# Pre-LN attention and mixture of experts on one core: late small clears, more places for w1, results in larger pieces, and another start of the first sequence

## The chip, the cores and the metric

One Trainium2 chip, of which the kernel uses one core. The metric is the device time of one execution in microseconds; a comparison takes the median of several runs. Five engines work side by side, each through its own instructions in order: PE (matmul), DVE (vector), ACT (scalar), POOL (GpSimd) and SP, which here only issues DMAs. A DMA is issued by SP, ACT or POOL and lands later; whoever needs its data waits for its semaphore.

## The reference

Eight sequences of 512 tokens of width 128 go through one attention layer and one mixture of experts, both with a layernorm ahead and a residual behind.

```python
x = x + attn(layernorm(x), Wq, Wk, Wv, Wo, bo)   # 16 heads of 8, causal softmax
x = x + ffn(layernorm(x), gate_w, w1, b1, w2, b2)
# ffn: probs = softmax(x @ gate_w.T); the best 2 of 8 experts for each token
#      hidden = relu(x @ w1[e] + b1[e])   (128 -> 512)
#      out_e  = hidden @ w2[e] + b2[e]    (512 -> 128)
#      y = sum over the two experts of prob * out_e
```

All arrays are float32.

## The kernel before

**Order of the work.** Seven generators (`setup`, `project`, `shifts`, `attend`, `route`, `experts`, `sums`) each yield the time at which their next step is due, in units of one sequence; a loop at the end always runs the generator that is due first. The order so written is kept on PE, ACT, DVE and SP (`ORDERED`); POOL's order is left to the scheduler. An engine that waits holds up everything written behind it. On SP, ACT and PE nothing overtakes.

**Attention.** For sequence b, `project` (yield b - 1.7 on) does the layernorm, q and k, and splits both into three bf16 parts (`part`). The parts go to DRAM (`to_dram`, L378) and come back arranged by head (`pack`, L390) into `q2_buf[b % 2]` and `k2_buf[b % 2]` (trace names q and k), 24 rows a part, so that a bf16 matmul over 72 rows gives scores of float32 quality. For b = 0 this is done in four groups of four heads. For each group SP issues two q writes and three q packs, ACT one k write, POOL three k packs; on SP the order is write q, pack q, group after group. For later sequences it is one group, all on SP.

`shifts` takes, for each group g of four heads, the scores (L479, with the mask added at L489) in six units of one or two PSUM tiles, DVE takes the maximum of each tile's rows (L502), and the negated maximum, as two bf16 parts, is transposed (L446), copied (L450) and put by a DMA into two more rows of q2 (L456), for b = 0 on ACT's queue, later on SP's. `attend` then computes the scores again with keys as rows (L635; now with the shift in them), exponentials on ACT (L641), the causal zeroes by POOL's affine select (L647), and the products with v (L565).

**Dummy matmuls.** `keep_warm(k)` issues matmuls of 128x256 on a zero tile whose result nobody reads: 40 while the first input is loaded, and 75 (L129) behind the first sequence's v.

**Routing.** `route` chooses the experts of a sequence and gives each token and choice a slot in `xs[k]`, a DRAM array with room for each of the eight experts; `scatter` (L900) writes the normalised rows there with eight indirect DMAs of POOL. Sequences 0 to 6 are group k = 0, sequence 7 is group 1. `dispatch` is called after sequences 1, 3, 5, 6 and 7 and gives out the tiles of 128 slots that are certain to be full (steps 0 to 2) or all that remain (steps 3 and 4). A row that was never written must look empty: the whole of `xs[1]` and the spare part of `xs[0]` are cleared in `setup`; in `xs[0]` the 640 rows (`NEW`) behind each expert's fill are cleared after sequence 5 (L880 to L891), eight DMAs of SP. The scatters that come after wait for them.

**Experts.** The five steps have 8, 16, 16, 23 and 15 tiles; "tile 3.5" is tile 5 of step 3. For each four tiles SP gathers the rows (`gather`, L1050), and for each tile it fetches the expert's w1, b1 and b2 as one row of 644 words a partition (`fetch_to`, L973, 322 KB). PE transposes (L1081), multiplies by w1 (ph, L1120), ACT and DVE add b1 and take relu (L1127, L1129), PE multiplies by w2 (py, L984), DVE adds b2 (yo, L988), and POOL stores each row to `ys[k]` at its token's place (L1019). Tiles whose four are due before 8 have w1 in five buffers (`wt`), the 42 later ones in six places in the q of even sequences, with four fetched ahead.

**Sums.** When all stores of a group have landed, `sums` loads two rows of results for each token (L1173, 256 KB a DMA, into the q of odd sequences), adds them, weighted, to x (L1199) and stores x (L1155). For group 0 the first three sequences are loaded at once, that is six DMAs; the next ones follow the sums.

Of the kernel before, what the change touches and what calls it, by code (L numbers as in the profile page):

```python
# [9 lines left out]
F32 = mybir.dt.float32  # L10
# [8 lines left out]
P = 128  # L19
# [5 lines left out]
def preln_attn_moe(ctx: ExitStack, tc: tile.TileContext, x, wq, wk, wv, wo, bo,  # L25
# [35 lines left out]
    nc = tc.nc  # L61
# [10 lines left out]
    LEAD = 0.55  # L72
    WARM = (40, 75)
    XB = 3
# [33 lines left out]

    NEW = 2 * P if len(GROUPS[0]) == 1 else T + P
    ROOM = (len(GROUPS[0]) * T + P, T)  # L110
# [10 lines left out]


    idle_bf = const.tile([P, 2 * P], BF16, tag="idlebf", name="idle_bf")
    V.memset(idle_bf, 0.0)

    def keep_warm(k):
        idle = ps_mm.tile([P, T], F32, tag="mm", name=f"idle_{k}")
        for _ in range(WARM[k]):
            nc.tensor.matmul(  # L129
                idle[:, : 2 * P], lhsT=idle_bf[:, :P], rhs=idle_bf, start=True, stop=True  # L130
            )
# [87 lines left out]
    def setup():  # L219
# [13 lines left out]
        for k in range(2):  # L233
# [3 lines left out]
            )  # L237
        for t in (place_no, token):
            nc.gpsimd.iota(
                t, pattern=[[P, t.shape[1]]], base=0, channel_multiplier=1,  # L240
                allow_small_or_imprecise_dtypes=True,
            )
# [76 lines left out]
    def project():  # L319
# [13 lines left out]
        arrange(0, G)  # L333
        keep_warm(0)
        for b in range(B):
# [47 lines left out]
            def pack(s, g):  # L383

                src = (q_parts, k_parts)[s]
                heads = H // src.shape[0]
                for r in range(3):
                    o = r if s == 0 else 0
                    place = (q2_buf, k2_buf)[s][b % 2][24 * r : 24 * r + 24, ts(g, heads)]
                    (nc.gpsimd if b == 0 and s == 1 else nc.sync).dma_start(  # L390
                        out=place,
                        in_=src[g, o : o + 3].rearrange("c d h t -> (c d) h t"),
                    )
# [10 lines left out]
            if b > 0:  # L404
                to_dram(0, 0)
                yield b - 1.18
                to_dram(1, 0)
            else:

                for g in range(G):  # L410
                    for s in range(2):
                        to_dram(s, g)
                        pack(s, g)
                yield b - 1.18
# [22 lines left out]
            if b == 0:  # L437
                keep_warm(1)


    def shifts():
# [20 lines left out]
        for b in range(B):  # L462
            for g in range(G):
# [6 lines left out]
                for pr in range(2):  # L470
                    n = 2 * g + pr
                    for i, unit in enumerate(S_UNITS):
                        yield t0 + (3 * pr + i) / 24
                        for v, bank in enumerate(unit):
# [23 lines left out]
                            else:  # L498
                                top, src = pm[:, :, pr, 8], ps.rearrange(
                                    "p (u k) -> p u k", u=2  # L500
                                )
                            nc.vector.tensor_reduce(top, src, AX.X, ALU.max)  # L502
                        if late:
                            late.pop(0)()
# [295 lines left out]
    def dispatch(s, soon):  # L800
# [66 lines left out]
        if not last:  # L867
# [6 lines left out]
            else:  # L874
                given[k] = const.tile([P, E], F32, tag=f"given{k}", name=f"given_{k}")
                V.tensor_copy(given[k], taken)
        if len(GROUPS[k]) > 1 and b == GROUPS[k][-2]:

            fill = small.tile([1, E], I32, tag="fill", name=f"fill_{s}", bufs=1)
            V.tensor_tensor(fill, pc[0:1, :E], room[k][0:1, :E], ALU.add)  # L880
            yield soon(3)
            found = [
                nc.values_load(
                    fill[0:1, e : e + 1], engines=[mybir.EngineType.SP],
                    min_val=e * ROOM[k], max_val=(e + 1) * ROOM[k] - NEW,
                    skip_runtime_bounds_check_because="an expert has room for all tokens",
                )
                for e in range(E)
            ]
            for e in range(E):  # L890
                nc.sync.dma_start(  # L891
                    out=xs[k][bass.ds(found[e], NEW)].rearrange("(p a) d -> p a d", p=P),
                    in_=empty.unsqueeze(1).to_broadcast([P, NEW // P, XROW]),
                )

    def scatter(k, b, t):
        sent = []
        for i in range(NT):
            for j in range(2):
                ins = nc.gpsimd.indirect_dma_start(  # L900
                    out=xs[k],
                    out_offset=bass.IndirectOffsetOnAxis(
                        ap=slot[b][:, j * NT + i : j * NT + i + 1], axis=0
                    ),
                    in_=xn2[b][:, i, :], in_offset=None,
                )
                in_order(ins)
                for other in sent + [a for o in GROUPS[k] if o < b for a in scatters[o]]:
                    tc.declare_no_dep(
                        ins.ins, other, reason="every token and choice has its own slot"  # L910
                    )
                for other in gathers[k]:
                    tc.declare_no_dep(
                        ins.ins, other, reason="no slot of a tile given out is written"
                    )
                sent.append(ins.ins)
                if (i, j) != (NT - 1, 1):
                    t += 0.045 if b == B - 1 else 0.055
                    yield t
        scatters[b] = sent  # L920

# [7 lines left out]
    def experts():  # L929
        tiles = [(s, i) for s, step in enumerate(STEPS) for i in range(step[2])]  # L930
        wt, yo, at, xg, to, expert = {}, {}, {}, {}, {}, {}

        spare_q = q2_buf[0].rearrange("p h t -> p (h t)").bitcast(F32)
        spare_k = k2_buf[0].rearrange("p h t -> p (h t)").bitcast(F32)
        WTS, XGS = H * T // 2 // WROW, H * T // 2 // (4 * XROW)
        fetched = [0, 0, 0]
# [6 lines left out]
        def after(s, i):  # L943
            return when(s, quad(s, i)[0]) >= B

        def ahead(s, i):
            return WTS - 2 if after(s, i) else 3

# [3 lines left out]
        def fetch_to(n):  # L952
            while fetched[0] < min(n, len(tiles)):
# [11 lines left out]
                if after(s, i):  # L965
                    wt[s, i] = spare_q[:, ts(fetched[1] % WTS, WROW)]
                    fetched[1] += 1
                else:
                    wt[s, i] = work.tile(
                        [P, WROW], F32, tag="wt", name=f"wt_{s}_{i}", bufs=5  # L970
                    )
# [63 lines left out]
        def gather(s, i):  # L1035
# [13 lines left out]
            for j in range(m):  # L1049
                ins = nc.sync.dma_start(  # L1050
                    out=t[:, j, :], in_=xs[k][bass.ds(found[j], P)]
                )
                assert all(o in scatters for o in GROUPS[k] if o <= b)
                for o in GROUPS[k]:
# [34 lines left out]
        def loads():  # L1089
            t = 0  # L1090
            for s, i in quads:
                t = max(t, when(s, i + 1) - (0.22 if after(s, i) else 0.28))
                yield t
                while s not in row_no or STEPS[s][1] not in scatters:
                    t += 0.01
                    yield t
                gather(s, i)
# [51 lines left out]
    def sums():  # L1149
# [10 lines left out]
        for k, group in enumerate(GROUPS):  # L1160
# [5 lines left out]
            def load(n):  # L1166
# [5 lines left out]
                for j in range(2):  # L1172
                    ins = (nc.scalar if last and j else nc.sync).dma_start(  # L1173
                        out=y[:, j],
                        in_=ys[k][j * NTOK + n * T : j * NTOK + (n + 1) * T].rearrange(
                            "(c p) d -> p c d", p=P
                        ),
# [9 lines left out]

            yield t
            for n in range(min(3, len(group))):
                load(n)  # L1190
            if not last:
                t += 0.05
            for n, b in enumerate(group):
                y = ys_sb[n]
                for c in range(NT):
                    t += 0.05 if last else 0.013
                    yield t
                    for j in range(2):
# [3 lines left out]
                        )  # L1202
                    store(0)
                    if c == 0 and n > 0 and n + 2 < len(group):
                        load(n + 2)
# [52 lines left out]
```

## Time and profile before

| | us |
|---|---|
| median of 14 runs | 646.41 |
| lowest and highest | 644.95, 650.56 |
| profiled execution | 645.77 |
| its span | 644.0 |
| PE, DVE busy in the span | 565.6, 435.3 |
| ACT, POOL busy in the span | 305.4, 291.2 |
| mean granted PE clock | 0.927 |

A timeline line gives start, duration, engine, source line, operation, output and input tile, and how many; in brackets stands the idle time of the engine before it and what ended it. SPq and ACTq are the issues of DMAs. PEclk is the clock granted to PE, as a share of full speed. In a table of windows each engine has its busy time and the number of its instructions.

### The profile page before, as it was taken

Reading aid. Unit: us, or ns where it says so; the run is one execution under the profiler, and the core shown is the slowest. Engines: PE = TensorE matmul, PEld = TensorE weight load, DVE = VectorE, ACT = ScalarE, POOL = GpSimd, SP = SyncE. Lnnn points to the kernel's source line nnn. Section 1 sums busy time; section 2 is a strip of 40 time slices with the busy share of each in tenths; the row PEclk is TensorE's granted clock in tenths of the full one; section 3 lists DMA queues with packets and bytes.
Section 4 is the critical chain, followed back from the end, with each engine's and each line's share of the span. In section 5 each row is a group of like instructions: output and inputs, shape, how many; then the busy total and the mean of one; then the engine's idle time right before and its main releaser. Section 6 shows DMA issues by size and latency. Waiting matters only on the chain. (4 is left out here: it accounts for less than half of the span.)

```text
span 644.0 us, 13373 instructions
## 1 busy us (share of the span) xinstructions
PE 565.6 (88%) x4312; PEld 365.7 (57%) x4312; DVE 435.3 (68%) x1410; ACT 305.4 (47%) x679; POOL 291.2 (45%) x480
## 2 busy tenths in 40 slices
PE   8788999999899998989899998998388989999680
PEld 6434445435445454655556664665246779999670
DVE  4476577897798978788798866897165245433484
ACT  3135366556465565545545654554145433544230
POOL 3523242445456334645654465352435643764241
PEclk9779599999899999999999998999679998999796
DMA  2546337537825704722552374229522563887893
GB/s 73 177 129 140 64 116 149 165 116 168 180 86 124 185 26 110 180 64 79 135 130 66 119 170 128 68 68 149 114 75 81 156 204 94 254 232 241 248 306 95
DMA packets 77096, 87.95 MB, mean 137 GB/s; under 512 B 10796, under 2 KB 62164, under 8 KB 76020
## 3 DMA queue, kind: packets, MB, share of 16 engines
q1 hardware_dynamic: 70676, 75.85, 46.5%
q0 software_dynamic: 5120, 10.56, 5.2%
q8 instruction: 35, 0.57, 0.4%
q10 hardware_dynamic: 1232, 0.69, 0.4%
q14 instruction: 33, 0.27, 0.1%
HBM read 61.14 MB, written 28.22 MB: 139 GB/s over the span
## 5 line engine op out<-in xcount | busy, mean ns | idle before, releaser
L502 DVE TENSOR_REDUCE pm<-s 128x1 f32<-128x512 f32 (+2 forms) x320 | 206.9, 682 | 65.1 <-PE s L489 64.5
L641 ACT ACTIVATE pt<-st 128x512 f32<-128x512 f32 x320 | 178.1, 599 | 114.9 <-PE st L635 99.7
L647 POOL TENSOR_SCALAR_AFFINE_SELECT pt<-pt 128x256 f32<-128x256 f32 x256 | 101.6, 410 | 197.1 <-ACT pt L641 190.9
L479 PE MATMUL s<-k,q 72*128 72x512 bf16 (+3 forms) x512 | 119.9, 314 | 9.9 <-ACT pt L641 4.5
L565 PE MATMUL po<-pt,va 128*9 128x512 f32 (+3 forms) x1024 | 109.2, 454 | 7.5 <-POOL pt L647 7.4
L635 PE MATMUL st<-q,k 74*128 74x384 bf16 (+3 forms) x512 | 110.4, 313 | 5.1 <-DVE pm L502 2.8
L1019 POOL DMA_INDIRECT ys<-yo,to x78 | 75.5, 968 | 69.8 <-DVE x L1199 23.0
L984 PE MATMUL py<-w_sb,hT 128*128 x624 | 86.6, 285 | 0.4 <-ACT hT L1127 0.4
L479 PEld LDWEIGHTS <-q 72*128 72x128 bf16 x512 | 47.8, 101 | 68.8 <-issue 53.5
L489 PE MATMUL s<-mask_bf,ident_bf 128*128 128x256 bf16 (+1 forms) x320 | 84.0, 262 | 0.0
L984 PEld LDWEIGHTS py<-w_sb,hT 128*128 128x128 f32 x624 | 79.4, 200 | 4.1 <-issue 2.3
L900 POOL DMA_INDIRECT xs<-xn_f,slot x64 | 62.5, 977 | 27.2 <-issue 13.2
L635 PEld LDWEIGHTS <-k 74*128 74x128 bf16 x512 | 46.9, 102 | 28.7 <-issue 15.1
L565 PEld LDWEIGHTS po<-pt,va 128*9 128x9 f32 x1024 | 24.1, 90 | 65.7 <-issue 30.9
L1127 ACT ACTIVATE hT<-ph,q 128x128 f32<-128x128 f32 x126 | 37.1, 365 | 49.3 <-PE ph L1120 41.9
L1120 PE MATMUL ph<-xgT,q 128*128 128x128 f32 x336 | 47.0, 286 | 11.5 <-DMA q<-wrows 11.1
L1120 PE MATMUL ph<-xgT,wt 128*128 128x128 f32 x288 | 41.7, 290 | 12.2 <-DMA wt<-wrows 12.2
L1120 PEld LDWEIGHTS ph<-xgT,q 128*128 128x128 f32 x336 | 42.4, 199 | 13.9 <-DMA q<-wrows 8.9
L1120 PEld LDWEIGHTS ph<-xgT,wt 128*128 128x128 f32 x288 | 36.5, 199 | 17.0 <-DMA wt<-wrows 12.8
L1129 DVE TENSOR_SCALAR hT<-ph,q 128x128 f32<-128x128 f32 x42 | 14.7, 350 | 42.5 <-ACT hT L1127 41.4
L489 PEld LDWEIGHTS <-ident_bf 128*128 128x128 bf16 x320 | 32.4, 101 | 3.9 <-issue 2.1
L1129 DVE TENSOR_SCALAR hT<-ph,wt 128x128 f32<-128x128 f32 x72 | 20.2, 342 | 19.8 <-PE ph L1120 19.8
(155 smaller groups left out, 604.0 us busy)
## 6 DMA issues: line engine op xcount, KB each, us to landing
q<-wrows SPq DMA_DIRECT2D x42, 322.0 KB
wt<-wrows SPq DMA_DIRECT2D x36, 322.0 KB
q<-qparts SPq DMA_DIRECT2D x21, 384.0 KB
k<-kparts SPq DMA_DIRECT2D x21, 384.0 KB
q<-ys SPq DMA_DIRECT2D x15, 256.0 KB
k<-xs SPq DMA_DIRECT2D x42, 65.0 KB
qparts<-part SPq DMA_DIRECT2D x7, 384.0 KB
kparts<-part SPq DMA_DIRECT2D x7, 384.0 KB
```

Source lines behind the costliest of these rows:

```text
L479: nc.tensor.matmul(ps[:, at : at + (t + 1) * P], lhsT=q2[:KS, 2 * n + u, ts(t, P)], rhs=k2[:KS, 2 * n + u, : (t + 1) * P], start=(at == 0) ...
L489: nc.tensor.matmul(dst, lhsT=ident_bf, rhs=mask_bf if i > 0 else mask_bf[:, 0, :], start=False, stop=True, skip_group_check=True,)
L502: nc.vector.tensor_reduce(top, src, AX.X, ALU.max)
L565: nc.tensor.matmul(po[32 * h : 32 * h + VC, j * P :], lhsT=va[:, j, HG * g + h, :], rhs=at_cols(pts[pr], unit, u, at, W), start=(first and ...
L635: nc.tensor.matmul(ps[:, at : at + T - j * P], lhsT=k2[: KS + 2, 2 * n + u, ts(j, P)], rhs=q2[: KS + 2, 2 * n + u, j * P :], start=(at == ...
L641: nc.scalar.activation(pt[:, v, :], ps, AF.Exp, scale=SCALE)
L647: selects[0] = nc.gpsimd.affine_select(out=d, in_=d, pattern=[[0, 2], [1, P]], compare_op=ALU.is_ge, fill=0.0, base=0, channel_multiplier=-1,)
L900: ins = nc.gpsimd.indirect_dma_start(out=xs[k], out_offset=bass.IndirectOffsetOnAxis(ap=slot[b][:, j * NT + i : j * NT + i + 1], axis=0), ...
L984: nc.tensor.matmul(py, lhsT=hT[:, c, :], rhs=w2_sb[:, bass.ds(at[s, i] + c * E * D, D)], start=(c == 0), stop=(c == FC - 1),)
L1019: ins = nc.gpsimd.indirect_dma_start(out=ys[k], out_offset=bass.IndirectOffsetOnAxis(ap=to[s, first][:, i - first : i - first + 1], axis=0 ...
L1120: nc.tensor.matmul(ph[:, ts(c, P)], lhsT=wt[s, i][:, ts(c, P)], rhs=turned[s, first][:, ts(i - first, P)], start=True, stop=True,)
L1127: nc.scalar.activation(hT[:, c, :], ph[:, ts(c, P)], AF.Relu, bias=bias)
```

## The change

It has five parts.

1. **Clears.** The clears of 640 rows for each expert after sequence 5 are gone. After sequence 6, the last of group 0, 128 rows behind each expert's fill are cleared. They are declared free of any order against the scatters of group 0, in both directions. On SP they stand between the w1 fetches of tiles 2.4 and 2.5.
2. **Places for w1.** The 42 late tiles have twelve places: six as before and six in the k of odd sequences. Up to nine are fetched ahead, a count that grows from four by one with each tile.
3. **Results.** A token's row in `ys` is now 4p + c for token c * 128 + p, so that a load reads 2048 bytes in one piece for each partition, where it read four of 512. `token` is made to match.
4. **Sums.** Two sequences are loaded first, in two steps of their own, and the others two ahead of the sums; for group 0 one store is held back. On SP the first result load now stands behind the w1 fetch of tile 4.10; before, it stood behind that of tile 4.5.
5. **The first sequence.** All its packs are issued by SP, in the order: the q writes of groups 0 and 1, packs of q and k of group 0, the q write of group 2, packs of group 1, and so on; ACT issues the k writes as before. After each unit of `shifts` that is due before time 0 four dummy matmuls follow: eleven units, 44 matmuls.

POOL's order, which the scheduler makes, differs in few places: four scatters of sequence 5 stand among the selects that they stood behind, and the rstd of sequences 2 and 6 comes behind two selects, or one, that it came ahead of.

```diff
-    NEW = 2 * P if len(GROUPS[0]) == 1 else T + P
...
-        for t in (place_no, token):
+        for t, by_tile, by_row in ((place_no, P, 1), (token, 1, NT)):
             nc.gpsimd.iota(
-                t, pattern=[[P, t.shape[1]]], base=0, channel_multiplier=1,
+                t, pattern=[[by_tile, t.shape[1]]], base=0, channel_multiplier=by_row,
...
-                    (nc.gpsimd if b == 0 and s == 1 else nc.sync).dma_start(
+                    nc.sync.dma_start(
...
                 for g in range(G):
+                    to_dram(1, g)
+                to_dram(0, 0)
+                for g in range(G):
+                    if g + 1 < G:
+                        to_dram(0, g + 1)
                     for s in range(2):
-                        to_dram(s, g)
                         pack(s, g)
...
+                        if t0 + (3 * pr + i) / 24 < 0:
+                            keep_warm(WARM[2], f"{g}_{pr}_{i}")
...
-        if len(GROUPS[k]) > 1 and b == GROUPS[k][-2]:
+        if k == 0 and last:
...
-            yield soon(3)
+            yield soon()
...
             for e in range(E):
-                nc.sync.dma_start(
-                    out=xs[k][bass.ds(found[e], NEW)].rearrange("(p a) d -> p a d", p=P),
-                    in_=empty.unsqueeze(1).to_broadcast([P, NEW // P, XROW]),
-                )
+                ins = nc.sync.dma_start(out=xs[k][bass.ds(found[e], P)], in_=empty)
+                for other in [a for o in GROUPS[k] for a in scatters.get(o, ())]:
+                    tc.declare_no_dep(
+                        ins.ins, other, reason="these slots are no token's"
+                    )
+                cleared.append(ins.ins)
...
-        WTS, XGS = H * T // 2 // WROW, H * T // 2 // (4 * XROW)
+        HALF, XGS = H * T // 2 // WROW, H * T // 2 // (4 * XROW)
+        WTS = 2 * HALF
...
-            return WTS - 2 if after(s, i) else 3
+            if not after(s, i):
+                return 3
+
+            late = [a for a in tiles if after(*a)].index((s, i))
+            return min(WTS - 3, WTS // 2 - 2 + late)
...
-                            "(c p) d -> p c d", p=P
+                            "(p c) d -> p c d", p=P
...
-            yield t
-            for n in range(min(3, len(group))):
+            for n in range(min(2, len(group))):
+                yield t
                 load(n)
-            if not last:
-                t += 0.05
+                t += 0.0 if last else 0.03
...
-                    store(0)
-                    if c == 0 and n > 0 and n + 2 < len(group):
+                    store(0 if last else 1)
+                    if c == 1 and n + 2 < len(group):
```

## The prediction

> **What bounds the kernel now.** I read the page's slices first, then busy time by windows of 4 us, then the timeline, SP's queue alone, at each place where PE is idle, and last the order of instructions of both kernels engine by engine.
>
> The slices (16.1 us each; rows PE, PEclk, DMA):
>
> ```profile
> PE   8788999999899998989899998998388989999680
> ...
> PEclk9779599999899999999999998999679998999796
> DMA  2546337537825704722552374229522563887893
> ```
>
> From 90 to 445 us PE is busy nine tenths at full clock, and no part of the change works there. Three places stand out: the start (PEclk 7, 7, 9, 5), slice 29 (PE 3, DMA 9) and the end.
>
> Slice 29, in the timeline:
>
> ```profile
> 435.08 10.90 SPq L891 DMA_DIRECT2D xs<-empty  x8
> ...
> 446.10 3.24 SPq L456 DMA_DIRECT2D q<-nmT  x2
> ...
> 449.60 1.91 SPq L973 DMA_DIRECT2D wt<-wrows  x3
> ...
> 457.66 2.07 PE L1120 MATMUL ph<-xgT,wt 128*128 128x128 f32 x8 [9.14 <-DMA wt<-wrows]
> ...
> 457.89 0.97 POOL L900 DMA_INDIRECT xs<-xn_f,slot  x1 [11.51 <-DMA q<-nmT]
> ...
> 464.41 0.87 PE L565 MATMUL po<-pt,va 128*9 128x256 f32 x4 [2.97 <-POOL pt L647]
> ```
>
> Eight clears hold SP for 10.9 us. The shift rows behind them (their nmT is done at 432.61) go out at 446.10, the w1 behind those at 449.60, and PE waits 9.14 us for it. POOL's scatters of sequence 5 wait for the clears to land, until 457.89; selects queue behind the scatters, and PE waits for one again (2.97 us).
>
> The end:
>
> ```profile
> 595.10 4.39 SPq L1173 DMA_DIRECT2D q<-ys  x6
> ...
> 599.75 1.10 SPq L973 DMA_DIRECT2D q<-wrows  x2
> ...
> 604.41 2.08 PE L1120 MATMUL ph<-xgT,q 128*128 128x128 f32 x8 [6.10 <-DMA q<-wrows]
> ```
>
> SP stands before the first result load until the last store of group 0 has landed, issues six loads, and only then tile 5's w1. PE is idle from 598.31 to 604.41 and runs at half clock to 608.
>
> The start:
>
> ```profile
> 11.75 8.35 PE L129 MATMUL idle<-idle_bf 128*128 128x256 bf16 x75
> ...
> 17.73 6.22 POOL L390 DMA_DIRECT2D k<-kparts  x12
> ...
> 22.67 0.38 PE L479 MATMUL s<-k,q 72*128 72x512 bf16 x1 [2.56 <-DMA k<-kparts]
> ```
>
> The dummies end at 20.10, the first scores wait for k until 22.67. The granted clock then is a half in three stretches: 24.3 to 34.5, 41.4 to 48.2 and 61.8 to 78.9.
>
> **The start, -5.5 us.** The order of SP becomes: q writes of groups 0 and 1, q and k packs of group 0, q write of group 2, and so on: 12 packs more on SP, 12 fewer on POOL. SP's q write goes out at 12.92, the first q pack at 14.73, the third ends at 17.35 (rows as now). Three k packs at 0.39 us each (a group of three takes 1.12 to 1.18) end by 18.7; the q write of 17.62 was landed by 20.72, 2.3 us after its end, so k lands near 20.9 and the first scores come 1.7 us earlier. Later groups: 24 packs and 4 writes at 0.4 us are 11 us more, to about 30; scores of group 1 need theirs at 31. Hence the packs are covered; behind them on SP stand x2 and the small loads (now 32.57), which come earlier too.
>
> Dummies: 11 units (t0 below 0: six of group 0, five of group 1) get 4 matmuls, 44 x 0.111 us (75 took 8.35) = 4.9 us of PE. They lie in DVE's shadow: 10 maxima of 0.606 us are 6.06 us a group (the row at 35.65), PE's own score work 3.2 us at full clock (twice 22.67 to 24.3) plus 2.7 us of dummies 5.9. Each dummy tile takes a ps_mm buffer, so it waits for ACT or DVE to have read the tile three before; by the order these readers are done, and I take 0 (at most 1 us each for the three that wait on ACT).
>
> Followed through at full clock: DVE runs unbroken from first scores to xn of sequence 1 (5.3 us as now), scores and q projections, which at half clock took 28.5 to 36 us, are no longer PE's limit, and nh of group 0 ends near 31.0 instead of 34.05. nmT's row DMA, now at 36.57, is then at 33.6: -3.0. From 41.4 to 47.6 PE is busy without a break at half clock; at full clock that is 3.1 us shorter, of which I take 2.5, since DVE is busy 3.48 us of 40 to 44. Sum -5.5, bounds 0 and -9. The third half-clock stretch I leave as it is: its cause (PE 70% busy in 58.4 to 61.8, 1.0 us of it idle behind a maximum) is not touched, though the order now puts two selects ahead of the rstd that blocked POOL until 61.59.
>
> The fall at 24.3 came after a stretch of 3.4 us in which PE was 48% busy with no pause over 1.8 us, the one at 61.8 with no pause over 1.0 us. The Trainium skill (TensorE: Matmul & The Clock Gate, Part 1) has the clock fall only after an idle window of about 3.4 us; by that the dummies would fill pauses that cost nothing. The rows speak against it, and it is a rival below.
>
> **The large clears go, -14.7 us.** From 448.3 to 468.66 PE executes what is 5 us of work at full clock (busy time times PEclk: 1.2, 1.2 and 2.1 us in the windows from 456, 460 and 464, and 0.5). Without the clears: the shift rows go at 432.7, w1 at 434, so ph runs at 448.4 and not 457.66; the scatters, which the order now puts between the selects before, are done by 450, so the select behind 464.41 runs near 450.9 and po near 451.4 (-13.0); what follows to 468.66 ran at half clock (3.4 us, -1.7). What is late next is the gate chain at 472 (PE 1.84 of 4 us), which moves along. Bounds: 9.1, the plain stall, and 16.
>
> **The small clears come, +2.5 us.** Eight of 128 rows, behind the w1 of tile 2.4 (third step, tile 4). In today's times: DVE's fill after rowno, 495.1; the eight register loads took from 432.25 to 435.08, 2.8 us; the issues as xs gathers of the same size (1.89 us for four) 3.8 us: to 501.6. Behind them wait w1 of 2.5 (now 491.0), landing near 504.4, against ph at 503.06: 1.4 us; then the gather, which now waits for the clears to land (503.8), then w1 of 2.6, landing near 508.6 against 506.35 plus 1.4: 2.3 us in all. POOL, whose scatters do not wait for these, goes on. Bounds 0 (PE idles 1.7 us between 508 and 520 anyway) and +6.
>
> A price by rows supports this: 5120 packets of 520 bytes become 1024. The Trainium skill (DMA: Bandwidth & Descriptors, Bandwidth) has a 64 KB transfer at 0.95 us, which for eight would be an estimate of 7.6 us of transfer; the sum would be 3 us worse. No row has this clear alone.
>
> **Twelve places for w1, -1.5 us.** PE idles 2.7 us from 540 to 596 (sum over the windows), mostly for w1. Up to nine ahead instead of four removes most: -1.5, bounds 0 and -3. The second six places lie in k of odd sequences, free after sequence 7's last st at 513.80; the first write there is behind the row at 524.65, so it waits for nothing.
>
> **The end, -7.0 us.** By the new order the first result load stands behind the w1 of tile 4.10, not 4.5. That place is free when tile 3.21 is done (591), before the stores land (594.98). So PE goes on at 598.3. Next late is DVE: from relu of tile 4.5 to that of 4.14 its queue has 42 sums, 9 relus, 9 yo and 10 small ones; by starts in the rows at 611 to 616 a pair of sums takes 0.65, a relu 0.26, a yo 0.20, a small one 0.19: 13.7+2.3+1.8+1.9 = 19.7 us, against PE's 9 x 1.79 + 0.9 = 17.0. From 599.0 that gives 618.7 for the relu now at 627.12: -8.4. The loads must keep up: 8.9 MB moved in 595 to 628, less five w1 (1.6 MB) now fetched earlier, is 7.3 MB in 23 us, 317 GB/s, where the best windows show 333 to 341. So I take -6 (bounds -2 and -8.4). The last ys load, 634.30 to 638.5, has 128 rows a load instead of 512: -1.0, bounds 0 and -2 (half its 4.2 us pass before data flows fast). The out stores of sequences 5 and 6 move behind that load on SP; the eight sums after it (2.9 us) cover their issue.
>
> **Sum:** -5.5 -14.7 +2.5 -1.5 -6 -1.0 = -26.2. The profiled execution took 645.77 us (span 644.0 and 1.8 around it), so 619.6; it lies 0.6 below the median of 646.41, so I predict a median of **620 us**.
>
> **Rivals.**
> 1. *The third half-clock stretch goes too.* For it: POOL's new order frees the selects of 62.61, and PE's 0.87 us wait there; against: the 1.0 us pause stays. PE is busy 15.5 us in it; half back, less DVE's limit (3.81 of 4 us from 68), is -6: **614**. Chance 0.2.
> 2. *The dummies do not hold the clock.* PE waits for xn between 25 and 27 us whatever stands before, and one low stretch suffices; at half clock 44 dummies cost 9.4 us, part of it bare. The start then gives +1 instead of -5.5: **626.5**. By the rule of the Trainium skill named above the dummies would do as little. Chance 0.16.
> 3. *The new clears take the place of the old wait, and more.* If a clear is paid by DMA and landing, not by rows, PE stands between tiles 2.5 and 2.6 for as long as the clears take, less 8 us of cover (495.1 to 503.06), plus 2.8 of register loads, 4.3 of fetch and 3.4 of half clock after. It exceeds the other gains (28.7) only from about 26 us of clearing; the old ones took 22.5 to the fetch behind them. At 30 us: **650**. Against it: gathers of this very size, 0.47 us each. Chance 0.04.
>
> **Chances.** Forecast 0.57, the rivals as above, 0.03 that the parts cancel. The range leaves out rival 3 and little else: the terms' likely errors (3 at the start, 3 at the clears, 3 at the end) and rivals 1 and 2 give 610 to 632. A measurement can tell 0.3%, 2 us: faster 0.93, same 0.03, slower 0.04.
>
> **What would show it.** First scores near 21 us; PEclk 9 in slices 2 to 3; no gap over 3 us on PE near 435 to 460; eight short clears on SP right after the fill, PE's wait before tiles 2.5 and 2.6 under 3 us; no idle PE after tile 4.4, DVE nearly full from 570 on. I am wrong if PE waits for a gather behind the clears, if the start shows half clock with dummies in it, or if the sums wait for ys.

## The result, and the profile after

The changed kernel takes 626.76 us (median of 10 runs, 621.65 to 632.64) against 647.07 for the kernel before (47 runs): a ratio of 0.968, interval 0.9655 to 0.971. Forecast were 620 in a range of 610 to 632. So 20 of the forecast 26 us came. Here and below a ratio leaves out the runs that lie more than 1.5% above the fastest of their kernel, while a median counts all of them. The profiled execution took 626.73, its span is 624.9: 19.1 less than before.

The slices of the page (15.6 us each):

```profile
PE   8789399999999999998989999899989698999980
...
PEclk9989689999979999998999999899988899999995
DMA  3724716825853742461265237422321477898783
```

The deep hole of slice 29 and the pause ahead of the end are gone; the 6 in slice 31 is the place of the small clears. The start has clock 8 in slice 2 and 9 in slice 3, where 9 was forecast for both, but also a new hole: slice 4 (62 to 78 us) has PE 3 and clock 6.

Where the 19.1 us come from is read by setting the same matmuls of both traces side by side (start in the changed kernel less start in the one before, at the scores with keys as rows, and at ph in the later part; negative is ahead). The times that name the stretches are of the trace before.

| stretch | at its start | at its end | change | forecast |
|---|---|---|---|---|
| start, to 67 | 0 | -5.6 | -5.6 | -5.5 |
| 67 to 71: PE waits for sequence 1's k | -5.6 | +4.2 | **+9.9** | 0 |
| 71 to 404 | +4.2 | +5.4 | +1.2 | 0 |
| 404 to 469: large clears gone | +5.4 | -10.6 | -16.0 | -14.7 |
| 469 to 502 | -10.6 | -11.5 | -0.9 | 0 |
| 502 to 506: small clears | -11.5 | -5.4 | +6.1 | +2.5 |
| 506 to 536 | -5.4 | -8.8 | -3.4 | 0 |
| 536 to 581: places for w1 | -8.8 | -11.4 | -2.6 | -1.5 |
| 581 to the end | -11.4 | -19.1 | -7.7 | -7.0 |

**The new hole.** The timeline of SP alone, from the start:

```profile
12.87 1.78 SPq L381 DMA_DIRECT2D qparts<-part  x4
17.38 1.15 SPq L393 DMA_DIRECT2D q<-qparts  x3
18.59 1.17 SPq L393 DMA_DIRECT2D k<-kparts  x3
...
28.01 1.55 SPq L393 DMA_DIRECT2D q<-qparts  x3
37.92 1.11 SPq L393 DMA_DIRECT2D k<-kparts  x3
...
44.40 0.91 SPq L381 DMA_DIRECT2D qparts<-part  x2
45.41 0.45 SPq L381 DMA_DIRECT2D kparts<-part  x1
55.32 2.04 SPq L393 DMA_DIRECT2D q<-qparts  x3
57.74 1.23 SPq L393 DMA_DIRECT2D k<-kparts  x3
```

The line at 37.92 is the last group's k packs, 8 us after the q packs ahead of them. The last two are the packs of sequence 1; in the trace before they stood at 45.45 and 48.68. SP's waits from 0 to 90 us say for what (total, times, longest):

```profile
SPq L393 <- DMA q<-nmT: 17.0, 3, 8.4
```

`q<-nmT` are the shift rows of sequence 0, which ACT issues. The packs of sequence 1 write another buffer and need none of them. What couples them is the instruction list: the DMAs of SP and ACT take eight semaphores in turn (called the ring below), and each waits until the one that had its semaphore last has landed. In the list the first q pack of sequence 1 has the semaphore of one shift row of the third group, and the first k pack that of the other; ACT issued these two rows at 53.66 and 54.21, and the pack went out at 55.32. A DMA of SP can so wait for one of ACT that has nothing to do with it, and that one waits for PE and DVE. Two lines of the windows (PE, PEld, DVE, ACT, POOL busy, PEclk, DMA share, GB/s) show that no transfer was in the way while SP stood, and one line of the timeline shows the price on PE:

```profile
48.00:52.00 4.00, 3.92 (x41) 1.81 (x39) 3.37 (x7) 2.37 (x5) 1.03 (x3) 1.00 0.02 7
52.00:56.00 4.00, 4.00 (x33) 1.99 (x29) 3.65 (x13) 3.17 (x7) 0.81 (x2) 1.00 0.03 6
```

```profile
72.62 0.59 PE L486 MATMUL s<-k,q 72*128 72x512 bf16 x1 [10.71 <-DMA k<-kparts]
```

The packs themselves, 144 packets of 16 KB, are under way for some 15 us in both traces (from 46.4 in the one before, from 56.2 here). So what PE loses in this step, 9.9 us, is the delay of their issue, 55.32 less 45.45.

**Clears.** The former place of the large clears, in the timeline of the changed kernel: shift rows and w1 go out at once, and ph is not waited for.

```profile
438.01 1.14 SPq L463 DMA_DIRECT2D q<-nmT  x2
...
439.39 6.54 SPq L996 DMA_DIRECT2D wt<-wrows  x3
...
453.73 1.05 PE L1143 MATMUL ph<-xgT,wt 128*128 128x128 f32 x8
```

The small clears, in the timeline from 480 us:

```profile
487.89 4.01 SPq L900 DMA_DIRECT2D xs<-empty  x8
...
492.18 0.35 SPq L996 DMA_DIRECT2D wt<-wrows  x1
...
495.46 1.91 SPq L1073 DMA_DIRECT2D xg<-xs  x4
...
495.97 1.91 PE L1143 MATMUL ph<-xgT,wt 128*128 128x128 f32 x8 [4.29 <-DMA wt<-wrows]
```

PE stands 4.29 us for the w1 of tile 2.5 and then runs at half clock to 499.5 (1.91 for a ph of 1.16). The kernel before has a half-clock window of the same length here too, from 498.7 to 502.2, which is the gain from -9.9 to -11.5 within the table's row 469 to 502; taken from 491 to 506, the small clears cost 3.9 us net.

**The end.** SP's timeline again: between the first result loads stand w1 fetches that nobody waits for yet; the last load is the one at 615.91.

```profile
583.36 0.81 SPq L1196 DMA_DIRECT2D q<-ys  x2
584.41 0.34 SPq L996 DMA_DIRECT2D q<-wrows  x1
584.80 0.91 SPq L1196 DMA_DIRECT2D q<-ys  x2
...
615.91 0.34 SPq L1196 DMA_DIRECT2D q<-ys  x1
```

In the table of windows PE has no pause from 576 to 596, and DVE is the full engine from 600 on:

```profile
588.00:592.00 4.00, 4.00 (x38) 4.00 (x38) 3.75 (x17) 2.34 (x8) 1.41 (x2) 1.00 0.96 282
...
600.00:604.00 4.00, 4.00 (x38) 4.00 (x37) 3.76 (x17) 1.77 (x6) 1.44 (x2) 1.00 1.05 372
604.00:608.00 4.00, 2.83 (x20) 2.32 (x20) 3.83 (x15) 0.88 (x3) 1.75 (x3) 1.00 0.40 122
```

### The profile page after: what moved, and what is told of

It reads as the page before. It is cut to its first block, busy times and chain, and to the rows that moved or that the text cites. A ratio compares the mean times of both kernels' runs of the same rounds, so it can differ in the third digit from the quotient of the medians.

```text
span 624.9 us, 13451 instructions
## 1 busy us (share of the span) xinstructions
PE 555.3 (89%) x4356; PEld 361.9 (58%) x4356; DVE 435.0 (70%) x1410; ACT 305.0 (49%) x679; POOL 285.2 (46%) x468
## 5 line engine op out<-in xcount | busy, mean ns | idle before, releaser
L486 PE MATMUL s<-k,q 72*128 72x512 bf16 (+3 forms) x512 | 116.6, 307 | 19.5 <-DMA k<-kparts 13.1
L644 PE MATMUL st<-q,k 74*128 74x384 bf16 (+3 forms) x512 | 108.6, 309 | 4.0 <-DVE pm L509 1.5
L574 PE MATMUL po<-pt,va 128*9 128x512 f32 (+3 forms) x1024 | 106.5, 447 | 3.3 <-POOL pt L656 3.2
L496 PE MATMUL s<-mask_bf,ident_bf 128*128 128x256 bf16 (+1 forms) x320 | 82.3, 257 | 0.0
L1007 PEld LDWEIGHTS py<-w_sb,hT 128*128 128x128 f32 x624 | 77.8, 196 | 7.2 <-issue 2.5
L644 PEld LDWEIGHTS <-k 74*128 74x128 bf16 x512 | 46.5, 102 | 27.1 <-issue 13.5
L1150 ACT ACTIVATE hT<-ph,q 128x128 f32<-128x128 f32 x72 | 21.2, 365 | 22.4 <-PE ph L1143 17.8
L1152 DVE TENSOR_SCALAR hT<-ph,wt 128x128 f32<-128x128 f32 x72 | 20.2, 342 | 15.9 <-PE ph L1143 15.6
L457 ACT COPY nmT<-nmTp 32x128 bf16<-32x128 bf16 x32 | 8.1, 253 | 44.5 <-PE nmTp L453 31.1
L1150 ACT ACTIVATE hT<-ph,wt 128x128 f32<-128x128 f32 x72 | 20.5, 367 | 15.0 <-PE ph L1143 7.6
L1221 DVE SCALAR_TENSOR_TENSOR x<-q,gate,x 128x128 f32<-128x128 f32 x64 | 21.5, 348 | 8.1 <-DMA q<-ys 7.0
```

Of the source, the lines that this page charges most:

```text
L486: nc.tensor.matmul(ps[:, at : at + (t + 1) * P], lhsT=q2[:KS, 2 * n + u, ts(t, P)], rhs=k2[:KS, 2 * n + u, : (t + 1) * P], start=(at == 0) ...
L496: nc.tensor.matmul(dst, lhsT=ident_bf, rhs=mask_bf if i > 0 else mask_bf[:, 0, :], start=False, stop=True, skip_group_check=True,)
L574: nc.tensor.matmul(po[32 * h : 32 * h + VC, j * P :], lhsT=va[:, j, HG * g + h, :], rhs=at_cols(pts[pr], unit, u, at, W), start=(first and ...
L644: nc.tensor.matmul(ps[:, at : at + T - j * P], lhsT=k2[: KS + 2, 2 * n + u, ts(j, P)], rhs=q2[: KS + 2, 2 * n + u, j * P :], start=(at == ...
L1007: nc.tensor.matmul(py, lhsT=hT[:, c, :], rhs=w2_sb[:, bass.ds(at[s, i] + c * E * D, D)], start=(c == 0), stop=(c == FC - 1),)
L1150: nc.scalar.activation(hT[:, c, :], ph[:, ts(c, P)], AF.Relu, bias=bias)
```

## The experiments

Theory after the result: the new start costs more than it brings because the ring of semaphores makes the packs of sequence 1 wait for shift rows of sequence 0. Its rival: the packs are late because twelve more stand in one queue's transfers. The twelve kernels ran in three groups, each group on one chip beside the kernel before. The median of that was 646.8 in the first group, 656.8 in the second and 655.8 in the third. In the traces of the last two, PE, ACT and DVE stand between 540 and 590 us at waits of which the profile shows no cause: ACT at some that end in "remote", DVE (2.5 to 9.9 us) and PE (1.2 to 7.8 us) at some that end in "issue". The traces of the first group and of the first runs have none of these there, and "issue" only on POOL, on ACT (up to 4.9 us) and before PE's weight loads (0.7). So kernels are compared by their ratio to before, and best within a group. The first group and the second have no runs of the changed kernel itself; in the third its ratio was 0.979 and not 0.968, so a difference of 1% between groups is not proof by itself. Where a trace is called so many us ahead or behind at some time, and nothing else is named, it is set against the trace of before from the first runs, and the time is of that trace.

**Shift rows on POOL** (first group).

```diff
-                (nc.scalar if b == 0 else nc.sync).dma_start(
+                (nc.gpsimd if b == 0 else nc.sync).dma_start(
```

> The changed kernel, with the shift rows of the first sequence issued by POOL instead of ACT, so that they leave the ring of eight semaphores that the DMAs of SP and ACT take in turn. Theory (ring): the packs of sequence 1 went out at 55.3 and not at 45.5 because their semaphores were still held by shift rows of the first sequence's third group; now they go out by 47, sequence 1's k is there by 62, PE's wait of 10.7 us at its scores is under 2 us, and the time is 613 to 619 us against 626.8. Rival (transfer): the packs are late because 12 packs more, 36 packets of small rows each, stand in one queue's transfers; then they still land after 66 and the time is 623 to 628. Eight issues of POOL, about 1 us each among its selects, may cost 1 to 2 us under either.

Measured: 0.960 (0.952 to 0.968), median 626.6 of widely spread runs (619.1 to 632.7). SP's timeline:

```profile
43.72 1.35 SPq L393 DMA_DIRECT2D q<-qparts  x3
45.31 1.10 SPq L393 DMA_DIRECT2D k<-kparts  x3
```

The packs of sequence 1 go out 11.6 us earlier, and PE doesn't wait for its k any more (its only long wait for a k is 4.1 us, before the first scores). The price on POOL was larger than expected: PE waits 3.97 and 2.13 us for shift rows.

**k packs on POOL** (first group).

```diff
-                    nc.sync.dma_start(
+                    (nc.gpsimd if b == 0 and s == 1 else nc.sync).dma_start(
                         out=place,
```

> The changed kernel, with the twelve k packs of the first sequence on POOL's queue again, their order in the text otherwise new. Theory (ring): twelve DMAs fewer pass through the ring, the packs of sequence 1 wait for nothing but their own writes and go out by 46; the wait of 10.7 us is gone; the first scores are at 22 to 23; 614 to 619 us. Rival (transfer): the same bytes move at the same time, the packs land late as before, 623 to 628.

Measured: 0.960 (0.953 to 0.967), median 621.3.

```profile
47.61 1.12 SPq L393 DMA_DIRECT2D q<-qparts  x3
48.79 1.29 SPq L393 DMA_DIRECT2D k<-kparts  x3
```

The wait is gone with the same bytes moved. Two repairs that have only the ring in common remove it; the rival has fallen. Between 67 and 71 us, where the five traces with the new start and dummies lose 9.6 to 11.9 us, the traces of all repaired starts, and of the old one, lose at most 0.3. But the first scores come at 24.59, not at 22 to 23, and at 67 us this trace stands 2.5 us behind the one before, where the changed kernel was 5.6 ahead: the repair gave head start back. How much is open: the trace of "Both repairs" below, with the same start, is 2.3 ahead at 67, and it has no half clock from 44.8 to 55.0, as this one has.

The ratios, 0.960 for either of the two repairs and 0.968 for the changed kernel in the first runs, have intervals that touch. A gain in time beyond the spread is shown by the third group, for both repairs together.

**No dummies** (first group).

```diff
-                        if t0 + (3 * pr + i) / 24 < 0:
-                            keep_warm(WARM[2], f"{g}_{pr}_{i}")
```

> The changed kernel without the 44 dummy matmuls beside the first sequence's maxima. Theory (the dummies hold the clock): the granted clock is a half from about 24 to 34 us again, the first shift rows go out 1 to 3 us later than 34.5, and the ring passes that on: 628 to 630. Rival (they do nothing, or cost what they take): full clock there all the same, or no later rows: 625.5 to 627.

Measured: 0.979 (0.973 to 0.986), median 633.3, which is above both forecasts. The clock is a half from 25.1 to 35.3, the first shift rows go out at 37.37 instead of 34.52, SP's packs of sequence 1 at 58.88 instead of 55.32, and PE's wait is there as before:

```profile
76.70 0.58 PE L486 MATMUL s<-k,q 72*128 72x512 bf16 x1 [11.23 <-DMA k<-kparts]
```

By the ratios the dummies would be worth some 1.1% in this kernel. The trace places only part of it: it is 4.1 us behind the changed kernel's at 71 us and 9.2 at 404, and in the 333 us between the two kernels do the same. What the dummies do is asked again below.

**Old start** (first group): the two edits above, and the old order of writes and packs.

```diff
                 for g in range(G):
-                    to_dram(1, g)
-                to_dram(0, 0)
-                for g in range(G):
-                    if g + 1 < G:
-                        to_dram(0, g + 1)
                     for s in range(2):
+                        to_dram(s, g)
                         pack(s, g)
```

> The changed kernel with all of part 5 undone: packs in the old order, the k packs on POOL, no dummies. The trace of the changed kernel stood 4.2 us behind that of before at 75 us and 5.4 at 450, so by the traces the time is 620.5 to 622.5. If the later gains hung on the phase that the new start gives them, 624 or more.

Measured: 0.961 (0.954 to 0.967), median 622.2: as the traces said. By the medians the whole of part 5 costs some 0.8%, 5 us; the intervals touch here too.

**Only the clears** (second group): the kernel before, with part 1 alone.

> The kernel before with part 1 alone: no clears of 640 rows after sequence 5, eight of 128 rows after sequence 6. By the two traces the large clears were worth 16.0 us (from 5.4 us behind to 10.6 ahead between 455 and 469) and the small ones cost 5.1 (11.5 ahead at 502, 5.4 ahead at 506): 635 to 637 us against 646.4. Rival: part of the 16 is not theirs but comes from another phase of the clock, whose half-clock stretches lie elsewhere in every execution: 638 to 641.

Measured: 0.9875 (0.983 to 0.992), median 647.6 against 656.8: 9 us less. The trace has both terms again: 1.3 us behind before at 400 us, 14.6 ahead at 469, 15.8 at 502 and 8.2 at 507. So -15.9 and +7.6. By its ratio the kernel would take 638 of the 646.4 us, which is at the edge of the rival's range and not in the theory's, and the interval, 635 to 641, holds both. For the theory speaks that all thirteen traces without the large clears gain 15.9 to 16.0 us between 404 and 469, though their half-clock windows lie differently; but they are all set against one trace of before, so its own half clock (451.0 to 461.2 and 464.6 to 468.0) stays untested.

**Clears later** (second group).

```diff
             V.tensor_tensor(fill, pc[0:1, :E], room[k][0:1, :E], ALU.add)
-            yield soon()
+            yield soon(6)
```

> The changed kernel with the small clears later on SP: behind the w1 fetches of tiles 2.5 and 2.6 and the gather between them, and not between the fetches of 2.4 and 2.5. Theory: PE's wait of 4.3 us for the w1 of tile 2.5 and the half clock behind it (1.7) are the price of the place on SP, not of the clearing; the w1 of 2.7, now behind them, is due 4 to 5 us later than that of 2.5 and is late by 1 at most: 622 to 624 us. Rival: the wait only moves to tile 2.7, 626 to 628.

Measured: 0.975 (0.967 to 0.983), median 641.4. The changed kernel, run in the third group under like conditions, has 0.979 (0.975 to 0.983); by the time alone this is inconclusive. By the changed kernel's clock, its trace is 2.2 us behind the changed kernel's at 480, 4.0 at 489, and 0.5 ahead at 501. Over all traces the gain is plainer: between 491 and 506 the nine kernels with the early clears lose 3.7 to 5.5 us, the four with the later ones between 2.3 and nothing. So the place on SP was most of the price. In this trace PE waits for no w1 between 470 and 530 us: the wait did not move to tile 2.7, as the rival has it.

**Six places** (second group).

```diff
-        WTS = 2 * HALF
+        WTS = HALF
...
-            return min(WTS - 3, WTS // 2 - 2 + late)
+            return WTS - 2
```

> The changed kernel with six places for the w1 of the late tiles and four fetched ahead, as before; all else new. Theory A: the end hangs on the places, since nine w1 fetched ahead carry PE over SP's stand before the first result load: the 2.6 us gained between 536 and 581 and some 5 of the 7.7 at the end are lost, 632 to 635. Theory B (the sums' new order carries the end): only the 2.6 are lost, 628.5 to 630.

Measured: 0.989 (0.984 to 0.995), median 649.6: 1% above the changed kernel of the third group. From 545 to 640 us PE waits for a w1 four times, 5.6 us in all. The timeline at the end:

```profile
602.84 0.81 SPq L1196 DMA_DIRECT2D q<-ys  x2
...
603.92 0.32 SPq L996 DMA_DIRECT2D q<-wrows  x1
...
608.29 1.16 PE L1143 MATMUL ph<-xgT,q 128*128 128x128 f32 x8 [3.01 <-DMA q<-wrows]
```

Here the w1 behind the first load is wanted soon, and PE stands for it. By the traces the loss is smaller than by the medians: from 548 us to the end this one loses 4.9 us against before, the changed kernel of the third group 2.4. The other 4.7 us by which the two differ are there at 548, ahead of most of the late tiles, and what brought them is not shown.

**Old order of the sums** (second group).

```diff
-            for n in range(min(2, len(group))):
-                yield t
+            yield t
+            for n in range(min(3, len(group))):
                 load(n)
-                t += 0.0 if last else 0.03
+            if not last:
+                t += 0.05
...
-                    store(0 if last else 1)
-                    if c == 1 and n + 2 < len(group):
+                    store(0)
+                    if c == 0 and n > 0 and n + 2 < len(group):
```

> The changed kernel with the old order of the sums: three sequences loaded at once, in one step, no store held back; twelve places for w1. Theory A (the end hangs on the places): 626 to 629, the w1 of the tiles up to 4.10 having been fetched before the first result load. Theory B (the sums' order carries it): PE stands before tile 4.5 or a later one for over 3 us, 631 to 634.

Measured: 0.980 (0.975 to 0.986), median 643.9: no difference from the changed kernel that can be told. From 545 us on PE waits for no w1 at all, though SP issues six loads at once ahead of one. So with the twelve places the order of the sums adds nothing that can be told (theory A). That does not make it worthless: from 548 us to the end this trace loses 1.8 us, six places with the new order 4.9, and "Only the clears", which has neither (nor the larger pieces), 9.3, with one wait of 6.9 us for a w1. The places bring all of it by themselves; the new order and the larger pieces bring over half when the places are missing.

**The changed kernel again** (third group).

> The changed kernel itself, as the base of this call, since the times of a kernel differ from call to call. Expected: a ratio to before of 0.966 to 0.971, as measured, and the wait of 10 to 11 us for sequence 1's k in its trace under every theory.

Measured: 0.979 (0.975 to 0.983), median 641.4 against 655.8. The ratio is worse than the 0.968 of the first runs: its median rose by 14.7 us and that of before by 8.8. Its trace loses 12.3 us against the first one from 548 us to the end, where the waits named above lie; before has no trace in this group to compare. PE's wait for sequence 1's k is 10.8 us, and up to 400 us this trace lies within 1 us of the first one at most places.

**Both repairs** (third group): k packs on POOL and clears later.

> The changed kernel with the first sequence's k packs on POOL's queue (which gave about 0.8% of the time of before) and the small clears behind the w1 fetches of tiles 2.5 and 2.6 and the gather between them (which by the trace gave 3 to 4 us at 500 us). Theory: the two are far apart and add up: 7 to 9 us faster than the changed kernel of this call. Rival: the later clears gain nothing, as the wait moves to tile 2.7 or is given back before the end, which stores and sums set: 4 to 6 us faster.

Measured: 0.962 (0.957 to 0.968), median 632.6: 8.8 us below the changed kernel of this group, with intervals that don't meet. The trace at the clears (timeline of SP, then of PE):

```profile
483.58 3.52 SPq L900 DMA_DIRECT2D xs<-empty  x8
487.38 3.38 SPq L996 DMA_DIRECT2D wt<-wrows  x2
```

```profile
486.25 2.08 PE L1143 MATMUL ph<-xgT,wt 128*128 128x128 f32 x8
...
491.23 1.06 PE L1143 MATMUL ph<-xgT,wt 128*128 128x128 f32 x8
```

No ph waits for a w1. This is faster than both kernels. The trace is 7.5 us ahead of the changed kernel's at the end; 5.4 are there at 404, from the start, and 2.2 more come at the clears, by 506.

**First group's k packs on SP** (third group).

```diff
-                    (nc.gpsimd if b == 0 and s == 1 else nc.sync).dma_start(
+                    (nc.gpsimd if b == 0 and s == 1 and g > 0 else nc.sync).dma_start(
```

> As the former, but the first group's three k packs stay on SP and only the nine of the later groups are on POOL. Theory: the first scores come 1 to 2 us earlier than with all on POOL and the ring still holds no pack of sequence 1: within 2 us of the former, rather faster. Rival: POOL's nine packs, issued early, slow the first group's packs all the same: no difference.

Measured: 0.963 (0.958 to 0.968), median 630.1. The same time; but the first scores come at 24.71, not earlier than the 23.83 with all on POOL. The theory of 1 to 2 us at the first scores fell, the rival stands.

**Both repairs, no dummies** (third group).

> The kernel with k packs on POOL and later clears, without the 44 dummy matmuls. Theory (the dummies hold the clock and that shortens the path by itself): 2 to 5 us slower than with them. Rival (the 6.5 us that their removal cost in the changed kernel came through the ring, which passed the late shift rows on to the packs of sequence 1): within 1.5 us, or faster, since without the ring's wait nothing follows the rows.

Measured: 0.961 (0.956 to 0.967), median 631.7: no difference from the same with dummies. The half clock lasts from 23.0 to 36.7 instead of 23.3 to 30.1, the first shift rows go out at 38.65 and 37.98. So if the dummies bring the 1.1% above, it is by way of the ring; these runs can't tell more. That they shorten the path by themselves is not shown; in these two traces it is 2.6 us at 404 us, and less than a measurement can tell at the end.

## Why the prediction was right in sign and 6 us off

The sum came out near, and partly by luck. In the table three rows are worse than forecast by 14.7 us together (the step at 67, the stretch behind it and the small clears), the others better by 7.5, and 3.4 of these are a stretch of half clock that had no part in the argument (point 7).

1. **Start: the step that failed.** "Hence the packs are covered; behind them on SP stand x2 and the small loads (now 32.57), which come earlier too." They came later: the last k packs at 37.92 and not by 30, x2 at 39.67 (before 33.18), the packs of sequence 1 at 55.32. I added up issue times and took SP to be free between them; each issue also waits for the DMA that had its semaphore before. (The sum itself was miscounted: behind group 0's packs come 18 packs and not 24, so by its own terms it gives 27.5 and not 30.) The waits were readable in the trace before, among SP's waits from 0 to 90 us:

```profile
SPq L257 <- DMA q<-nmT: 12.2, 1, 12.2
...
SPq L390 <- DMA q<-nmT: 7.3, 2, 5.2
```

The first is harmless, since nothing urgent was behind it; the second are packs of sequence 1 (L390) that already waited for shift rows. Twelve DMAs more on SP made that wait longer and put the last k packs behind another. What it cost: 9.9 us in one step, +4.2 instead of -5.5. The gain up to 67 us was right to 0.1, but not by my terms: first scores at 22.42 (forecast 20.9: the first q pack went at 17.38 and not 14.73, since with four q writes ahead of it it came to the semaphore of ACT's first k write and stood 2.6 us for it, the ring again), shift rows 2.05 earlier (forecast 3.0), half clock only in 42.1 to 45.6 in place of 41.4 to 48.2 and with no stretch at 24. The five traces with this start and the dummies are 3.8 to 5.7 us ahead at 67, so the head start is no accident of one execution; their first shift rows go out from 34.52 to 37.51 (before 36.57), so the 2.05 us are.

2. **Third half-clock stretch.** Forecast to stay, and it did, but for another cause: PE is at half clock from 66.0 to 83.1, now behind the new wait. So this trace tests neither the forecast nor rival 1. Without that wait the traces differ: 67.6 to 77.9 in "Both repairs", none with the first group's k packs on SP.
3. **Dummies (rival 2).** The clock was full from 24 to 34 in the first trace with them, but not in the others: between 20 and 39 us the nine traces with dummies have 0 to 6.8 us of half clock, the five without 10.2 to 13.7. So the dummies shorten it and do not hold the clock, and a half clock with dummies in it, which the prediction named as a sign of being wrong, came in eight of nine. The rival is refuted as to the clock; in time no difference can be told once the ring is out of the way. The Trainium skill (TensorE: Matmul & The Clock Gate, Part 1) lists half clock as the state after at least one idle window of about 3.4 us; "only" was the prediction's reading of it. This trace shows that a fall needs no idle window: the clock fell at 42.1 after a window of 3.41 us in which PE was 75% busy and paused for 0.37 us at most.
4. **Large clears.** -16.0 in one pair of traces and -15.9 in the other, against -14.7 and at the end of its bounds: right in place and near in size. That the half clock was the undersized part is likely and not shown.
5. **Small clears.** The mechanism was the forecast one (w1 of tile 2.5 behind eight issues), the size not: +6.1, just past the upper bound, or +3.9 net of the half clock that before had here. The issues ended at 491.9, against 491.4 as worked out (501.6 less the 10.2 us gained so far). But the w1 took 3.8 us to land and not 2.8, and the stall of 4.29 us, which was to be under 3, brought 3.4 us of half clock, which the term did not count. The Trainium skill (DMA: Bandwidth & Descriptors, Bandwidth) has 0.95 us for a 64 KB transfer, measured on loads that GpSimd issued; here the 1024 packets took 28 ns each (median), some 0.22 us a clear on 16 engines, less than the 0.5 us from one issue to the next. The measured packets decide; the place on SP was most of the cost. Rival 3 didn't come.
6. **Places and end.** -2.6 and -7.7 against -1.5 and -7.0. The cause was as told (w1 fetched beyond the first load, DVE next: 3.8 of 4 us from 600 on), but the prediction gave the whole of the end to the order of the sums, and the twelve places alone suffice for it: without the order nothing that can be told is lost, without the places part of it (2.5 to 3.1 us by the traces, 1% by the medians). The last load to the end took 9.0 us against 9.8, forecast -1.0.
7. **Not forecast:** -3.4 between 506 and 536, where before ran at half clock from 529.5 to 536.3 and the changed kernel did not. That is luck: the twelve other traces have anything from -3.4 to +0.4 there, and three of them, with the same parts in this stretch, show half clock in the same place.

What stays open: whether a start with all k packs on SP and without the ring's wait would keep the 5.6 us. The repairs tried gave half of them or more back in other ways. Open too is what the engines wait for between 540 and 590 us in the last two groups.

## What to carry to other kernels

Before moving DMAs to another queue, ask which semaphore each takes and who had it before: a transfer that depends on nothing can be held by one that waits for the compute engines, and the engine's queue behind it stands too. Price an inserted step on a queue by what is wanted next behind it, not by its own duration, and add the half clock that a stall brings. When several edits share an end, undo them one at a time and also together: here one part carried the end alone, another, made for the same purpose, added nothing to it and yet brought over half where the first was missing. And set several traces of the same code against each other before a gain of 2 or 3 us is called the work of an edit.

## What the runs showed of the hardware that I had not expected

- **The clock has a grid of its own.** In every trace all changes of the granted clock lie on a grid of 3.413 us, and the grid stands differently against the kernel's start in each execution: 0.40 us in the trace before, 1.18 in the changed kernel's, 3.20 in its repeat. The same kernel had a stretch from 42.1 to 45.6 in one execution and from 23.7 to 27.1 in the other.
- **Times of one kernel scatter** (changed: 621.65 to 632.64, 1.8% from end to end), and the slowest has the lowest mean clock (0.938 at 632.64, 0.954 at 621.65). I take the grid for the cause; no run could hold it fixed.
- **How busy PE was in a grid window does not decide by itself:** in the changed kernel the clock stayed full after windows of 53% and 63% (from 18.3 and from 25.1 us), and fell after one of 75% (from 38.7).
- **Larger pieces in the result loads** are read at 84 ns per 2048 bytes, where four packets of 512 took 27 each: a fifth less.
